# Fourth query product by Strassen's scheme in matmuls of 128 columns, in the scores' bank; another order of the products; an input ring of four

## The chip, the core and the metric

The kernel runs on one core of a Trainium2 chip. The core has a matrix engine (TensorE, "PE" in the profile; its weight loads are a row of their own, "PEld"), three engines for elementwise work (VectorE "DVE", ScalarE "ACT", GpSimd "POOL") and a queue for transfers (SyncE, "SP"). Each engine works through its own instructions in the order in which the program issues them, and waits where an instruction needs something that is not there yet. Matmuls write into eight banks of accumulators, which VectorE and ScalarE read. The metric is the device time of one execution in microseconds.

## The reference

One layer of attention with shared keys and values is added to its input. `x` is 64 batches of 128 tokens with 512 features in fp32; there are 16 heads of 64.

```python
xn = layernorm(x, g_in)
q = (xn @ Wq).reshape(b, n, H, DH).transpose(0, 2, 1, 3) * scale
kv = xn @ Wkv
k, v = (kv[..., :DH], kv[..., DH:])
...
k = jnp.concatenate([nk, k], axis=1)
v = jnp.concatenate([nv, v], axis=1)
sim = jnp.einsum('bhid,bjd->bhij', q, k)
...
sim = sim + bias
...
attn = jax.nn.softmax(sim, axis=-1)
out = jnp.einsum('bhij,bjd->bhid', attn, v)
out = out.transpose(0, 2, 1, 3).reshape(b, n, INNER)
out = out @ Wo
return layernorm(out, g_out)
```

The caller adds `x` to the result. A causal mask and a mask of keys set entries of `sim` to a large negative number, and one extra key and value (`nk`, `nv`) stand in front. The part that the change touches is `xn @ Wq`: a product of 512 features with 1024 query columns.

## The kernel before

**Groups and pairs.** Four batches make a group (`GB`), whose 512 tokens are projected together; two batches make a pair, and the main loop runs over pairs `d`. One pass of the loop is `turn(d)` and then `body(d)`; the text calls it a half, since two of them project one group. `turn(d)` makes the scores of batches 2d and 2d+1 (`scores`, L652), adds them to the bias rows (`scores_add`), and multiplies the transposed weights of the pair before with the values (`values`, L781). `body(d)` projects half of the query columns of group d // 2 + 1, runs the softmax of its pair (`exps` on ScalarE, `rinv` on VectorE, `scale` on GpSimd, `blocks_T`, a transpose on VectorE), and makes the output projection and the layer norm of earlier pairs (`out_product`, L868, `pair_norm`). `turn_end`, `body_end` and `body_last` do the last pairs. Even d is the first half of a group (h = 0) and also makes its token sums on GpSimd (`token_sum`, L497, `token_sums_inner`, L560 to 562). The order of the work is written out by hand: each engine's queue is the order of the calls.

**The query product.** The 512 x 512 blocks of weights and tokens are multiplied by Strassen's scheme in Winograd's form: seven products in place of eight (`product`, L515), each of two matmuls with 256 columns per chunk of 128 query columns. A half has two chunks, f0 and f1. Partial sums stay in accumulators: bank "a" takes products 1, 6, 7, 4 in turn (`keep` copies it out in between on ScalarE, L527), bank "c" takes 5 and 3, and `q_out` writes the queries `qT` (L536 on VectorE, L533 on ScalarE). From d = 2 on the second of the seven products is itself made by the same scheme, for both chunks of a half at once: seven matmuls of 128 columns (`inner_product`, L581, tile `pl`, in bank "w") in place of four of 256, with seven adds on VectorE (`inner_out`, L597). Its weight sums are made once, its token sums once a group.

**The values.** `values` works in four strips s of 32 rows and two halves r of columns, eight places of the array in turn. Per batch a strip does one matmul of 256 columns and three of 128. The parameter `wide` names strips that do two of the short ones as one; no call uses it.

**Banks and buffers.** Bank pair "s" (`ps_s`) holds, within a half, the scores of the first batch, then `pkv`, then a normed output row (`yn`, even batch) until `pair_residual` (L932) has read it. The input rows `x` go through a ring of `XB` = 5 tiles; the masks through two tiles, loaded by `load_mask` at h = 0.

**Start.** `q_half` and `q_batches` project the first group without Strassen's scheme; `q_batches` works batch by batch in matmuls of 128 columns. `values_T` transposes a group's values at the end of its second half, ahead of the last `exps` of the first batch.

Of the kernel before, what the change touches and what calls it, by code (L numbers as in the profile page):

```python
# [17 lines left out]
def kernel(  # L18
# [81 lines left out]
    NEG = -1.0e38  # L100
    XB = 5
    assert N == P and DH == 64 and TOK == 512
# [12 lines left out]
    def load_x(m, queue=nc.sync):  # L115
        g, t = divmod(m, GB)
        pool, tag = (rp, "res") if m in (XB, XB + 1) else (xp, "x")
        xs[m] = pool.tile([P, DIM], FP, tag=tag, name=f"x_{m}")
        if g < 2:
            queue.dma_start(out=xs[m], in_=x[m])  # L120
        else:
            nc.sync.dma_start(
                out=xs[m], in_=x[g * GB : (g + 1) * GB, t * Q : (t + 1) * Q, :]
            )

    def load_res(b):
        pool, tag = (rp, "res")
        if b >= B - 6:
# [17 lines left out]
    nkv = const.tile([P, 1], FP, name="nkv")  # L146
    nkv_neg = const.tile([P, 1], FP, name="nkv_neg")
    nbp = const.tile([P, R8], FP, name="nbp")
# [18 lines left out]
    gin_rows = const.tile([KC, P], FP, name="gin_rows")  # L167
    nc.scalar.dma_start(out=gin_rows, in_=g_in.rearrange("(kc p) -> kc p", p=P))
# [70 lines left out]

    ident = const.tile([P, P], FP, name="ident")  # L240
    make_identity(nc, ident)
# [130 lines left out]
    def null_negative():  # L372
        nc.vector.tensor_scalar(nkv_neg, nkv, -1.0, None, ALU.mult)

    def kv_pair_out(m, pkv):
# [13 lines left out]
        for at, to, n in ((0, 0, 2), (3, 2, 1), (2, 3, 1)):  # L389
# [3 lines left out]
                AF.Identity,  # L393
                bias=nkv_neg[K_ROWS],
            )
# [194 lines left out]
    def inner_out(g, h, f, t, at, name=None):  # L590
# [6 lines left out]
        nc.vector.tensor_tensor(o, p, k, ALU.add)  # L597

    S, nmax, rsum = {}, {}, {}

# [138 lines left out]
    def values_rooms_apart(p):  # L739
# [18 lines left out]
            ps_y.tile(shape, FP, tag="X", name=f"po_{p + 1}_3"),  # L758
        ]

    def values(b, wide=()):
# [194 lines left out]
    def turn(d):  # L956
# [15 lines left out]
        po = values_rooms(p)  # L972
        values(p)
        values(p + 1)
        if d % 2 and (d + 1) // 2 < NG:
# [49 lines left out]
    def body_first():  # L1025
# [19 lines left out]
        tokens_T(m)  # L1045
        load_mask(g + 1)
        for f in range(2):
# [197 lines left out]
    def body(d):  # L1245
# [8 lines left out]
        f0, f1 = 2 * h, 2 * h + 1  # L1254
        deep = q and d > 1

        if q:
# [68 lines left out]
        if q:  # L1326
            product(g, f0, 7, ps_q, "a", start=False)
            keep("a", "u3")
            q_out(g, HC + f0, 1, "c", "u3")
        if ln:  # L1330
# [5 lines left out]
        if soft:  # L1336
            scale(b, 0)
        if xw:
            norm_apply(m)
# [12 lines left out]
        if soft:  # L1352
            exps(a, 1, 0, 1)
        if q:
            product(g, f0, 4, ps_q, "a", start=False)
            q_out(g, HC + f0, 0, "a")
            product(g, f0, 3, ps_q, "c", start=False)
            q_out(g, f0, 1, "c", "u2")
# [14 lines left out]
        if soft:  # L1373
            exps(a, 1, 1, 4)
        if q:
            product(g, f1, 1, ps_q, "a")
            keep("a", "p1")
        if deep:
            inner_product(g, h, 7)
            inner_out(g, h, 1, 1, 0, "p1")  # L1380
            inner_out(g, h, 1, 1, 1)
        elif q:
            q_out(g, f1, 0, "w", "p1")
            weight_sums_inner()
        if q and h == 1:
            values_T(g)
        if soft:
# [3 lines left out]
            exps(b, 1, 0, 2)  # L1391
        if q:
            product(g, f1, 5, ps_q, "c")
        if out:
            out_product(p, 5, ps_y, "Y")
            out_keep("Y", "yp5", "yp5")
        if soft:
            exps(b, 1, 2, 3)
# [3 lines left out]
        if deep:  # L1402
            inner_product(g, h, 4)
            inner_product(g, h, 3)
            inner_out(g, h, 1, 0, 0, "p1")
            inner_out(g, h, 0, 1, 1)
        if soft:
            exps(b, 1, 3)
            blocks_T(a)
# [6 lines left out]
        if q:  # L1416
            product(g, f1, 7, ps_q, "a", start=False)
            keep("a", "u3")
            q_out(g, HC + f1, 1, "c", "u3")
        bias_add(b + 2)  # L1420
# [5 lines left out]
        if q:  # L1426
            product(g, f1, 3, ps_q, "c", start=False)
            q_out(g, f1, 1, "c", "u2")
        if out:
            pair_stats(p)  # L1430
            pair_pow(p)
            out_product(p, 7, ps_y, "X", start=False)
            out_part(p + 1, 1, "X", "yp5")
        if soft:
            blocks_T(b)
        if q:
            product(g, f1, 4, ps_q, "a", start=False)
            q_out(g, HC + f1, 0, "a")
        if out:
            out_product(p, 4, ps_y, "X", start=False)  # L1440
# [73 lines left out]
    bias_add(0, (slice(0, UK.start), slice(UK.start, ROW)))  # L1514
    q_batches((7,))
    norm_T(7)
# [104 lines left out]
```

## Time and profile before

| | |
|---|---|
| time, median of 3 runs | 1027.39 us (1027.23 to 1027.47) |
| the profiled execution's own time | 1027.63 us |
| span of its profile | 1025.8 us |
| TensorE busy | 1016.4 us |
| VectorE, ScalarE, GpSimd busy | 800.4, 697.4, 744.7 us |
| moved by DMA | 100.84 MB, 98 GB/s |

Times in the rows are microseconds from the start of the span unless marked ns. A row of a timeline gives start, length, engine, line, operation, what is written `<-` what is read, the shape, and in brackets the idle time of the engine just before it with what ended it. The ends of matmuls are modelled, and they overlap; the distance from one start to the next is what a matmul costs in a stream.

### The profile page before, as it was taken

How to read it: one execution, taken by the hardware profiler on the slowest of the kernel's cores; microseconds unless marked ns; L12 is line 12 of the kernel's file. 1: busy time of each engine (PE TensorE's matmuls, PEld its weight loads, DVE VectorE, ACT ScalarE, POOL GpSimd, SP SyncE). 2: the span in 40 equal slices, each digit the busy share in tenths (PEclk: the TensorE clock that was granted, in tenths of full speed). 3: DMA queues.
4: the chain of work that ended last, by engine and by line, in shares of the span. 5: the costliest groups of instructions: out<-in, count | busy, mean ns of one | idle time of the engine just before them, and what ended most of it. 6: DMA issues, size and time to landing. Idle time of an engine off the chain costs nothing.

```text
span 1025.8 us, 31271 instructions
## 1 busy us (share of the span) xinstructions
PE 1016.4 (99%) x12345; PEld 898.9 (88%) x12345; DVE 800.4 (78%) x1774; ACT 697.4 (68%) x2805; POOL 744.7 (73%) x579
## 2 busy tenths in 40 slices
PE   9999999999999999999999999999999999999997
PEld 9888888888888888888888888888888888888886
DVE  6877788877778877788777888777887777877697
ACT  5765678666677666786666776666776667856582
POOL 4997768676686867759677686766868678586676
PEclk9999999999999999999999999999999999999999
DMA  7415243051431414224052330514314152140211
GB/s 217 139 30 150 69 117 120 30 155 64 143 97 66 125 56 150 89 81 137 29 165 74 109 123 26 165 63 138 103 51 130 64 151 89 70 113 21 88 64 62
DMA packets 73833, 100.84 MB, mean 98 GB/s; under 512 B 32212, under 2 KB 36056, under 8 KB 71896
## 3 DMA queue, kind: packets, MB, share of 16 engines
q1 hardware_dynamic: 73392, 98.47, 30.9%
q8 instruction: 96, 1.57, 0.7%
q14 instruction: 49, 0.40, 0.1%
q10 hardware_dynamic: 296, 0.40, 0.1%
HBM read 63.19 MB, written 33.55 MB: 94 GB/s over the span
## 4 chain that ended last, share of the span: by engine, by line
PE 97%; DVE 1%; POOL 1%; issue 0%; POOLq 0%; DVEq 0%; ACT 0%
PE pa L515 20%; PE pyX L868 19%; PE pyY L868 10%; PE pc L515 10%; PE po L781 7%; PE pkv L363 6%; PE pyw L868 5%; PE pl L581 4%; PE pq L450 3%; PE ps L652 3%; PE sc_X L652 2%; PE sc_Y L652 2%; PE py_s L868 1%; PE sc_a L652 1%; PE busy L1453 1%; PE sc_w L652 1%
## 5 line engine op out<-in xcount | busy, mean ns | idle before, releaser
L683 ACT ACTIVATE s<-s,nmax 128x65 f32<-128x65 f32 (+1 forms) x1024 | 372.2, 368 | 62.1 <-DVE nmax L674 62.0
L705 POOL TENSOR_TENSOR s<-s,rinv 128x512 f32<-128x512 f32 (+1 forms) x132 | 190.6, 1446 | 159.9 <-DVE rinv L701 159.9
L617 POOL TENSOR_TENSOR s<-biasp,mneg 128x1552 f32<-128x1552 f32 (+1 forms) x65 | 206.0, 3171 | 51.1 <-DVE s L667 38.1
L683 ACT ACTIVATION_READ_ACCUMULATOR s<-s,nmax 128x1 f32 x1024 | 195.4, 191 | 0.0
L533 ACT COPY qT<-pa 128x256 f32<-128x256 f32 x59 | 22.0, 373 | 147.7 <-PE pa L515 147.7
L674 DVE TENSOR_REDUCE nmax<-s 128x8 f32<-128x1032 f32 (+1 forms) x128 | 121.4, 949 | 0.1
L515 PE MATMUL pa<-xS,wq 128*128 128x256 f32 x472 | 121.2, 379 | 0.0
L721 DVE STREAM_TRANSPOSE sb<-s 128x1536 f32<-128x1536 f32 (+1 forms) x68 | 113.5, 1672 | 2.0 <-POOL s L705 2.0
L868 PE MATMUL pyX<-wo,oT 128*128 128x256 f32 x464 | 109.7, 379 | 0.0
L868 PE MATMUL pyX<-wT,oT 128*128 128x256 f32 x464 | 109.7, 379 | 0.0
L515 PEld LDWEIGHTS pa<-xS,wq 128*128 128x128 f32 x472 | 87.3, 190 | 11.0 <-issue 0.2
L868 PEld LDWEIGHTS pyX<-wo,oT 128*128 128x128 f32 x464 | 86.0, 190 | 10.5
L868 PEld LDWEIGHTS pyX<-wT,oT 128*128 128x128 f32 x464 | 85.9, 190 | 10.6
L848 POOL TENSOR_TENSOR oT<-oT 128x512 f32<-128x512 f32 x64 | 80.5, 1276 | 3.9 <-PE pyw L868 1.6
L781 PE MATMUL po<-sb,vr 32*64 32x256 f32 (+1 forms) x4064 | 81.0, 300 | 0.0
L781 PEld LDWEIGHTS po<-sb,vr 32*64 32x64 f32 x4064 | 70.9, 130 | 8.1 <-issue 5.7
L536 DVE TENSOR_TENSOR qT<-pc,ku 128x256 f32<-128x256 f32 x118 | 48.6, 412 | 35.9 <-PE pc L515 20.8
L597 DVE TENSOR_TENSOR qT<-pl,kp 128x128 f32<-128x128 f32 x112 | 31.3, 280 | 55.5 <-PE pl L581 52.9
L800 ACT ACTIVATE oT<-po,nv 128x512 f32<-128x512 f32 (+1 forms) x127 | 73.8, 655 | 0.1
L281 POOL TENSOR_TENSOR rstd<-rstd,nhalf 128x1 f32<-128x1 f32 x64 | 35.0, 554 | 42.1 <-DVE rstd L280 39.2
L527 ACT COPY ku<-pa 128x256 f32<-128x256 f32 x118 | 43.4, 368 | 30.2 <-PE pa L515 26.2
L363 PE MATMUL pkv<-xT,wkv 128*128 128x256 f32 x256 | 63.3, 391 | 0.0
(186 smaller groups left out, 2418.9 us busy)
## 6 DMA issues: line engine op xcount, KB each, us to landing
res<-in_x_dram SPq DMA_DIRECT2D x64, 256.0 KB
x<-in_x_dram SPq DMA_DIRECT2D x63, 256.0 KB
out_dram<-y SPq DMA_DIRECT2D x63, 256.0 KB
xd<-xb SPq DMA_DIRECT2D x14, 1024.0 KB
xT<-xd SPq DMA_DIRECT2D x56, 256.0 KB
vr<-vd SPq DMA_DIRECT2D x64, 128.0 KB
kT<-kT SPq DMA_DIRECT2D x32, 64.0 KB
vd<-vb SPq DMA_DIRECT2D x32, 64.0 KB
```

The costliest lines, as they stand in the source:

```text
L363: nc.tensor.matmul(pkv, wkv[:, kc, :], xT[g][:, t : t + 2, kc, :], start=(kc == 0), stop=(kc == KC - 1),)
L515: nc.tensor.matmul(prod[tag], w[:, kc, f * P : (f + 1) * P], t[:, :, kc, :], start=(start and kc == 0), stop=(kc == HK - 1), skip_group_ch ...
L617: nc.gpsimd.tensor_tensor(S[b][:, :, keys], biasp[:, :, keys], mneg[:, t, keys] .unsqueeze(1) .broadcast_to([P, R8, keys.stop - keys.start ...
L652: nc.tensor.matmul(home[r][u * DH : (u + 1) * DH, f, :], qT[g, f, t // 2][rows, t % 2, hf, u], kT[rows, 0 : nk // Q, t, :], start=True, st ...
L674: nc.vector.tensor_reduce(nmax[b][:, hf], S[b][:, :, WITH_NULL[hf]], AX.X, ALU.max, negate=True)
L683: nc.scalar.activation(row, row, AF.Exp, bias=nmax[b][:, hf, k : k + 1], accum_out=rsum[b][:, hf, k : k + 1],)
L705: nc.gpsimd.tensor_tensor(sv, sv, rinvs[b, hf][:, lo:hi].unsqueeze(2).broadcast_to([P, hi - lo, sv.shape[2]]), ALU.mult,)
L721: nc.vector.transpose(sbs[b][:, :, lo:hi].rearrange("p j e q -> p e j q"), S[b][:, lo:hi, 1 : ROW - 1].rearrange("p e (j k) -> p e j k", k=Q),
L781: nc.tensor.matmul(po[s][rows, to : to + n], vr[g][quad, t, PLACE[j], :], sb[quad, slots, r * NF : (r + 1) * NF, :], start=(turn == 0), st ...
L800: nc.scalar.activation(to, src, AF.Identity, bias=nv2)
L848: eng.tensor_tensor(o, a, b, op)
L868: nc.tensor.matmul(prod[key], h[:, c, :], w[:, c, :], start=(start and c == 0), stop=(c == HC - 1), skip_group_check=not start,)
```

## The change

The fourth of the seven products gets the same treatment as the second, from d = 4 on (`deeper`): seven matmuls of 128 columns per half (`last_product`, tile `pm`) in place of the four of 256 of `product` 4, in the bank pair "s", which is free in that part of the body. Three weight sums lie in new tiles `wM` and `wR` (the tile `wM` first takes the fifth input row, `wR` the identity and `g_in`), the fourth overwrites a weight block; they are made at d = 2 and 3. The token sums (`token_sums_last`) are four subtractions on GpSimd per group, behind `scale(b, 0)` in the first half. In each half seven adds on VectorE (`last_out`) write the queries in place of two copies on ScalarE. `product` 1 of chunk f1 moves ahead into the place of product 4 of f0, and `product` 3 of f1 moves behind `out_product` 7. `values_T` goes behind `rinv` and `scale` of the first batch. From d = 5 on strip 3 of `values` is wide: for the first batch of a pair always, for the second at odd d and at d = 14 and 24. The input ring shrinks to four, the masks to one tile, loaded at h = 1. The last projection of the start is one `q_half`.

```diff
@@ constants and buffers
-    XB = 5
+    XB = 4
...
-        pool, tag = (rp, "res") if m in (XB, XB + 1) else (xp, "x")
-        xs[m] = pool.tile([P, DIM], FP, tag=tag, name=f"x_{m}")
+        pool, tag = (rp, "res") if m in (XB + 1, XB + 2) else (xp, "x")
+        xs[m] = wM if m == XB else pool.tile([P, DIM], FP, tag=tag, name=f"x_{m}")
...
-        m8s[g] = gp.tile([P, TOK], U8, tag="m8", name=f"m8_{g}")
+        m8s[g] = gp.tile([P, TOK], U8, tag="m8", name=f"m8_{g}", bufs=1)
...
+    wM = const.tile([P, DIM], FP, name="wM")
+    wR = const.tile([P, 2, P], FP, name="wR")
+    ident, gin_rows = wR[:, 0], wR[0:KC, 1]
@@ new functions
+    in_last = a22.rearrange("p k (h f m) -> p k f h m", h=2, f=2)
+    g11, g12 = in_last[:, 0, 0], in_last[:, 1, 0]
+    g21, g22 = in_last[:, 0, 1], in_last[:, 1, 1]
...
+    def token_sums_last(g):
+        b = xS[g, 4]
+        x = xM[g] = gp.tile([P, 3, N], FP, tag="xM", name=f"xM_{g}", bufs=1)
+        for o, p, m in (
+            (x[:, 0], b[:, 1, 0], b[:, 0, 0]),
+            (b[:, 1, 0], b[:, 1, 1], b[:, 1, 0]),
+            (x[:, 1], b[:, 1, 1], x[:, 0]),
+            (x[:, 2], b[:, 0, 1], x[:, 1]),
+        ):
+            nc.gpsimd.tensor_tensor(o, p, m, ALU.subtract)
...
+    def last_product(g, h, k):
+        if k == 1:
+            last_in[g, h] = ps_s.tile([P, 2, DIM], FP, tag="s", name=f"pm_{g}_{h}")
+        b, x = xS[g, 4], xM[g]
+        w, t, at = {
+            1: (g11, b[:, 0, 0], 0),
+            2: (g12, b[:, 0, 1], 2),
+            3: (v4, b[:, 1, 1], 1),
+            4: (g22, x[:, 2], 0),
+            5: (v1, x[:, 0], 1),
+            6: (v2, x[:, 1], 0),
+            7: (v3, b[:, 1, 0], 0),
+        }[k]
+        nc.tensor.matmul(
+            last_area(g, h, at),
+            w[:, h],
+            t,
+            start=k in (1, 2),
...
+    def last_out(g, h, f, t, at, first=False):
+        o = q_part(g, HC + 2 * h + f, 0)[:, t]
+        p = last_area(g, h, at).rearrange("p (h i) -> p h i", h=2)
+        k = o
+        if first:
+            k = base[f].rearrange("p (t h i) -> p t h i", t=2, h=2)[:, t]
+        nc.vector.tensor_tensor(o, p, k, ALU.add)
@@ turn
-        values(p)
-        values(p + 1)
+        values(p, WIDE if 4 < d < PAIRS - 1 else ())
+        values(p + 1, WIDE if 4 < d < PAIRS - 1 and (d % 2 or d % 10 == 4) else ())
@@ body
+        deeper = q and d > 3
...
-        if h == 0 and g + 1 < NG:
+        if h == 1 and g + 1 < NG:
             load_mask(g + 1)
...
+        if sums and d > 2:
+            token_sums_last(g)
...
-        if q:
+        if deeper:
+            product(g, f1, 1, ps_q, "a")
+        elif q:
             product(g, f0, 4, ps_q, "a", start=False)
             q_out(g, HC + f0, 0, "a")
...
+        if deeper:
+            last_product(g, h, 1)
+            last_product(g, h, 2)
...
-        if q and h == 1:
-            values_T(g)
+        if d == 2:
+            weight_sums_last(1, 2, 4)
         if soft:
             exps(a, 1, 4)
             rinv(a, 1)
             scale(a, 1)
             exps(b, 1, 0, 2)
+        if q and h == 1:
+            values_T(g)
...
+        if deeper:
+            last_product(g, h, 6)
+            last_product(g, h, 5)
+            last_out(g, h, 0, 1, 0, True)
...
+        if deeper:
+            product(g, f1, 3, ps_q, "c", start=False)
+            q_out(g, f1, 1, "c", "u2")
+            last_product(g, h, 3)
+            last_product(g, h, 4)
+            last_out(g, h, 1, 0, 0, True)
+            last_out(g, h, 0, 1, 1)
         if soft:
             blocks_T(b)
@@ start
-    q_batches((7,))
+    q_half(7, 0)
```

On TensorE, in the last third of `body(16)`, from the second `pyX` product to the last (`pa`, `pc` are query products of chunk f1, `pl` the inner product, `pyX`, `pyY` the output projection). Before:

```order
L868 MATMUL pyX_1_7161<-wT,oT_7076 128x256 x4
L515 MATMUL pa_1_1_7231<-xS_9_7106,wq 128x256 x2
L868 MATMUL pyY_5_7251<-wo,oT_7076 128x256 x4
L515 MATMUL pc_1_5_7248<-xT_6797,wS 128x256 x2
L868 MATMUL pyX_1_7161<-wo,oT_7076 128x256 x4
L515 MATMUL pa_1_1_7231<-xS_9_7159,wq 128x256 x2
L868 MATMUL pyX_1_7161<-wT,oT_7076 128x256 x4
```

And in the changed program:

```order
L647 MATMUL pm_0_7334<-xM_7297,wM 128x128 x2
L936 MATMUL pyX_1_7257<-wT,oT_7174 128x256 x4
L515 MATMUL pa_1_1_7312<-xS_9_7204,wq 128x256 x2
L647 MATMUL pm_0_7334<-xS_9_7255,wq 128x128
L936 MATMUL pyY_5_7351<-wo,oT_7174 128x256 x4
L936 MATMUL pyX_1_7257<-wo,oT_7174 128x256 x4
L515 MATMUL pc_1_5_7358<-xT_6888,wS 128x256 x2
L647 MATMUL pm_0_7334<-xS_9_7255,wR 128x128
L647 MATMUL pm_0_7334<-xM_7297,wq 128x128
L936 MATMUL pyX_1_7257<-wT,oT_7174 128x256 x4
```

Product 4 of f1 (`pa` from `xS_9_7159`) is gone; `pm` products 6 and 5, 7, 3 and 4 stand in between, and `pc` (product 3) and the last two `pm` are now the last ahead of the final `pyX`.

On VectorE, the end of the same half, from the second `rinv` to the last transpose. Before:

```order
L701 RECIPROCAL rinv_1_7280<-rsum_7153 128x8
L536 TENSOR_TENSOR qT_1_1_7084<-pc_1_5_7248,ku_7285 128x4x64
L898 TENSOR_TENSOR y_7197<-pyY_5_7251,kyu_7278 128x256
L536 TENSOR_TENSOR qT_1_1_7084<-pc_1_5_7248,ku_7261 128x4x64
L904 BN_STATS sto_7298<-y_7197 128x6
L906 BN_AGGR mvo_7300<-sto_7298 128x2
L908 TENSOR_SCALAR rstdo_7302<-mvo_7300 128x1
L898 TENSOR_TENSOR y_7309<-pyX_1_7161,kyp_7256 128x256
L721 STREAM_TRANSPOSE sb_7311<-s_6880 128x8x6x32
```

And in the changed program:

```order
L767 RECIPROCAL rinv_1_7386<-rsum_7249 128x8
L536 TENSOR_TENSOR qT_1_1_7182<-pc_1_5_7358,ku_7391 128x4x64
L663 TENSOR_TENSOR qT_1_0_7181<-pm_0_7334,ku_7391 128x2x64
L663 TENSOR_TENSOR qT_1_0_7181<-pm_0_7334,qT_1_0_7181 128x2x64
L966 TENSOR_TENSOR y_7293<-pyY_5_7351,kyu_7384 128x256
L972 BN_STATS sto_7404<-y_7293 128x6
L974 BN_AGGR mvo_7406<-sto_7404 128x2
L976 TENSOR_SCALAR rstdo_7408<-mvo_7406 128x1
L966 TENSOR_TENSOR y_7415<-pyX_1_7257,kyp_7356 128x256
L536 TENSOR_TENSOR qT_1_1_7182<-pc_1_5_7358,ku_7364 128x4x64
L663 TENSOR_TENSOR qT_1_0_7181<-pm_0_7334,ku_7391 128x2x64
L663 TENSOR_TENSOR qT_0_0_7179<-pm_0_7334,qT_0_0_7179 128x2x64
```

The transpose `blocks_T(b)` (L787 there) follows the last of these rows: the add of product 3 and two of the new adds, which need the last query products of the half, now stand ahead of it.

On TensorE in the changed `turn(16)`, the first batch's value products (`po_3` is strip 3):

```order
L849 MATMUL po_2_7095<-sb_6960,vr_6094 64x128 x2
L849 MATMUL po_3_7096<-sb_6960,vr_6094 64x2x128 x2
L849 MATMUL po_0_7093<-sb_6960,vr_6094 64x128 x2
L849 MATMUL po_1_7094<-sb_6960,vr_6094 64x128 x2
L849 MATMUL po_2_7095<-sb_6960,vr_6094 64x128 x2
L849 MATMUL po_0_7093<-sb_6960,vr_6094 64x128 x2
```

In the second turn strip 3 has a matmul of 2 x 128 columns, and in the third it has none.

More of the change, by code (lines that the diff above doesn't have):

```diff
@@ L597, in inner_out, with weight_sums_last, last_area @@
         nc.vector.tensor_tensor(o, p, k, ALU.add)
+    in_last = a22.rearrange("p k (h f m) -> p k f h m", h=2, f=2)
+    g11, g12 = in_last[:, 0, 0], in_last[:, 1, 0]
+    g21, g22 = in_last[:, 0, 1], in_last[:, 1, 1]
+    v1, v2 = (wM[:, i * 2 * P : (i + 1) * 2 * P] for i in range(2))
+    v1, v2 = (v.rearrange("p (h m) -> p h m", h=2) for v in (v1, v2))
+    v4, v3 = wR, g21
+    xM, last_in, base = {}, {}, {}
+    def weight_sums_last(*ks):
+        for k in ks:
+            o, p, m, op = {
+                1: (v1, g21, g22, ALU.add),
+                2: (v2, v1, g11, ALU.subtract),
+                4: (v4, g12, v2, ALU.subtract),
+                3: (v3, g11, g21, ALU.subtract),
+            }[k]
+            nc.vector.tensor_tensor(o, p, m, op)
+    def token_sums_last(g):
[8 more added lines that the diff above has]
+            nc.gpsimd.tensor_tensor(o, p, m, ALU.subtract)
+    def last_area(g, h, at):
+        two = last_in[g, h]
+        return two[:, 0, 0:N] if at == 0 else two[:, 1, (at - 1) * N : at * N]
+    def last_product(g, h, k):
[10 more added lines that the diff above has]
+            7: (v3, b[:, 1, 0], 0),
+        }[k]
+        nc.tensor.matmul(
[3 more added lines that the diff above has]
+            start=k in (1, 2),
+            stop=True,
+            skip_group_check=k not in (1, 2),
+        )
+    def last_out(g, h, f, t, at, first=False):
[5 more added lines that the diff above has]
+        nc.vector.tensor_tensor(o, p, k, ALU.add)
     S, nmax, rsum = {}, {}, {}
@@ L759, in values_rooms_apart @@
         ]
+    WIDE = (3,)
     def values(b, wide=()):
@@ L1045, in body_first @@
         tokens_T(m)
-        load_mask(g + 1)
         for f in range(2):
@@ L1374, in body @@
             exps(a, 1, 1, 4)
+        if q and not deeper:
+            product(g, f1, 1, ps_q, "a")
         if q:
-            product(g, f1, 1, ps_q, "a")
             keep("a", "p1")
+        if deeper:
+            last_product(g, h, 1)
+            last_product(g, h, 2)
         if deep:
             inner_product(g, h, 7)
+        if deeper:
+            last_out(g, h, 0, 0, 0, True)
+            last_out(g, h, 0, 0, 2)
+        if deep:
             inner_out(g, h, 1, 1, 0, "p1")
@@ L1391, in body @@
             exps(b, 1, 0, 2)
-        if q:
+        if q and h == 1:
+            values_T(g)
+        if q and not deeper:
             product(g, f1, 5, ps_q, "c")
@@ L1396, in body @@
             out_keep("Y", "yp5", "yp5")
+        if deeper:
+            product(g, f1, 5, ps_q, "c")
         if soft:
@@ L1425, in body @@
             out_part(p, 1, "Y", "yu2")
-        if q:
+        if q and not deeper:
             product(g, f1, 3, ps_q, "c", start=False)
@@ L1433, in body @@
             out_part(p + 1, 1, "X", "yp5")
+        if deeper:
+            product(g, f1, 3, ps_q, "c", start=False)
[4 more added lines that the diff above has]
+            last_out(g, h, 0, 1, 1)
         if soft:
             blocks_T(b)
-        if q:
+        if q and not deeper:
             product(g, f1, 4, ps_q, "a", start=False)
             q_out(g, HC + f1, 0, "a")
+        if d == 3:
+            weight_sums_last(3)
         if out:
```

17 lines of the change are left out of this document (11 added, 6 removed).

## The prediction

> **What bounds the kernel now.** I read the page first: busy shares, the granted clock, and the chain of work that ended last.
>
> ```profile
> span 1025.8 us, 31271 instructions
> ...
> PE 1016.4 (99%) x12345; PEld 898.9 (88%) x12345; DVE 800.4 (78%) x1774; ACT 697.4 (68%) x2805; POOL 744.7 (73%) x579
> ...
> PEclk9999999999999999999999999999999999999999
> ...
> PE 97%; DVE 1%; POOL 1%; issue 0%; POOLq 0%; DVEq 0%; ACT 0%
> ```
>
> TensorE is busy 99% of the span at full clock, and 97% of the chain is TensorE's own work. A busy share can hide waits, so the waits of TensorE come next, all of them in the whole span:
>
> ```profile
> PE py_s L868 <- DVE oT L798: 1.4, 2, 0.8
> PE busy L1453 <- POOL neg L245: 1.4, 1, 1.4
> PE pyc L868 <- DVE y L898: 0.6, 1, 0.6
> PE pc L515 <- DVE qT L536: 0.4, 1, 0.4
> ```
>
> That is 3.8 us, all at the start, in the second pair and in the last pairs. In the steady part TensorE waits for nothing. The third view cuts two consecutive halves (one `turn` plus one `body`) out of the steady part, from one start of the value products to the next, the odd d = 15 first and the even d = 16 second:
>
> ```profile
> 501.63:532.86 31.23, 31.23 (x387) 27.63 (x383) 25.00 (x57) 21.26 (x87) 21.28 (x15) 1.00 0.41 120
> 532.86:564.09 31.23, 31.23 (x387) 27.63 (x384) 24.28 (x56) 22.28 (x89) 24.00 (x22) 1.00 0.23 79
> ```
>
> The columns are length, then busy time of PE, PEld, DVE, ACT and POOL. A half lasts 31.23 us because TensorE has 31.23 us to do; VectorE has 6 to 7 us to spare in it, ScalarE 9 to 10, GpSimd 7 to 10. So a matmul taken out shortens the run by its own spacing, as long as the others still deliver in time.
>
> **The change, part by part.** The spacing is read from the even half, in order of time on TensorE. A matmul is two records, so "x4" is one product of two matmuls and "x2" one matmul; a stretch runs from one row's start to the next row's.
>
> ```profile
> 532.86 2.52 PE L781 MATMUL po<-sb,vr 32*64 32x256 f32 x128
> 535.31 1.99 PE L363 MATMUL pkv<-xT,wkv 128*128 128x256 f32 x8
> ...
> 538.00 0.38 PE L581 MATMUL pl<-xT,wq 128*128 128x128 f32 x2
> 538.22 1.89 PE L868 MATMUL pyX<-wo,oT 128*128 128x256 f32 x8
> ...
> 544.27 0.61 PE L581 MATMUL pl<-xL,wL 128*128 128x128 f32 x4
> 544.71 0.39 PE L581 MATMUL pl<-xT,wq 128*128 128x128 f32 x2
> 544.94 1.03 PE L515 MATMUL pa<-xS,wq 128*128 128x256 f32 x4
> 545.80 1.03 PE L515 MATMUL pc<-xT,wS 128*128 128x256 f32 x4
> ...
> 547.53 0.38 PE L581 MATMUL pl<-xL,wq 128*128 128x128 f32 x2
> 547.75 1.03 PE L515 MATMUL pc<-xS,wS 128*128 128x256 f32 x4
> ...
> 551.21 0.39 PE L581 MATMUL pl<-xL,wq 128*128 128x128 f32 x2
> 551.43 0.39 PE L581 MATMUL pl<-xT,wL 128*128 128x128 f32 x2
> 551.65 1.89 PE L868 MATMUL pyX<-wT,oT 128*128 128x256 f32 x8
> ...
> 558.56 1.03 PE L515 MATMUL pa<-xS,wq 128*128 128x256 f32 x4
> 559.42 1.89 PE L868 MATMUL pyX<-wT,oT 128*128 128x256 f32 x8
> ```
>
> *Term 1, the fourth product.* Removed in each half with d from 4 to 29 are product 4 of both chunks: the `pa` rows at 544.94 and 558.56, 0.86 us each, 1.72 us. Added are seven matmuls of 128 columns, which the second product already has in the same form: 0.22 (at 538.00), 0.67 for three (544.27 to 544.94), 0.22 (547.53) and 0.44 for two (551.21 to 551.65), 1.55 us. The half gets 0.17 us shorter; rows to 10 ns leave 0.17 to 0.18. Over 26 halves that is 4.4 to 4.7 us; I take 4.5.
>
> By these rows a matmul of half the columns costs half (0.22 against 0.43 us). [...]
>
> *Term 2, the wide value products.* In 41 calls of `values` (26 first batches, 15 second ones) strip 3 does two 128-column matmuls of each half of the rows as one of 256. Two matmuls fewer a call, the same columns. The two batches of the even half:
>
> ```profile
> 532.86:533.99 1.13, 1.13 (x62) 1.06 (x67) 1.00 0.32 112
> 533.99:535.31 1.32, 1.32 (x85) 1.15 (x67) 1.00 0.22 50
> ```
>
> 64 matmuls in 2.45 us are 38 ns each, so the most that two can give is 0.077 us a call, 3.1 us in all. But a strip streams 640 columns a batch, and at 0.43 us for 256 that alone is 1.08 us: the first batch (1.13) is already at its columns, and only the second (1.32, with the end of the stage in it) has something above them. The other end is a loss: if the other strips had to wait for the long matmul, 0.22 us a call. Between them I take 15 ns a call, 0.6 us in all, because the row nearest to it, the first batch, sits 0.05 us above its columns.
>
> *Term 3, the start.* The 0.4 us wait of TensorE in the second pair goes:
>
> ```profile
> L401 DVE STREAM_TRANSPOSE vb<-vT 64x512 f32<-64x512 f32 x16 | 11.3, 708 | 0.5
> 84.95 1.78 DVE L721 STREAM_TRANSPOSE sb<-s 128x1536 f32<-128x1536 f32 x1 [2.02 <-POOL s L705]
> 87.49 1.13 PE L515 MATMUL pc<-xT,wS 128*128 128x256 f32 x4 [0.45 <-DVE qT L536]
> ```
>
> There VectorE's `blocks_T(a)` waited 2.02 us for GpSimd's `scale`, which follows `rinv`, and that stood behind the 0.71 us of `values_T`. Now `rinv` goes first, and 0.45 us of lateness is less than 0.71. `q_half(7, 0)` also makes eight short matmuls into four long ones: 8 x 0.22 against 4 x 0.43, 0.05 us. I take 0.4 for both; the bounds are 0 and 0.5.
>
> *What must stay hidden.* VectorE gets seven adds a half, ScalarE loses two copies, GpSimd gets four subtractions in an even half. Two groups of instructions (mean ns of one behind the comma) and the timeline of the even half:
>
> ```profile
> L597 DVE TENSOR_TENSOR qT<-pl,kp 128x128 f32<-128x128 f32 x112 | 31.3, 280 | 55.5 <-PE pl L581 52.9 <-ACT kp L527 1.8
> L561 POOL TENSOR_TENSOR xL<-xT,xL 128x128 f32<-128x128 f32 x14 | 6.4, 457 | 1.1
> 559.10 1.77 DVE L721 STREAM_TRANSPOSE sb<-s 128x1536 f32<-128x1536 f32 x1
> 562.00 0.42 DVE L667 TENSOR_TENSOR s<-sc_w,s 128x256 f32<-128x256 f32 x1 [1.14 <-PE sc_w L652]
> 529.72 3.22 POOL L617 TENSOR_TENSOR s<-biasp,mneg 128x1552 f32<-128x1552 f32 x1 [0.84 <-DVE sb L721]
> 535.91 1.05 POOL L705 TENSOR_TENSOR s<-s,rinv 128x512 f32<-128x512 f32 x1 [0.38 <-DVE rinv L701]
> 539.20 1.27 POOL L497 TENSOR_TENSOR xS<-xT 128x512 f32<-128x512 f32 x1
> 541.68 1.03 PE L515 MATMUL pa<-xS,wq 128*128 128x256 f32 x4
> 543.68 0.69 DVE L932 TENSOR_TENSOR y<-yn,res 128x512 f32<-128x512 f32 x1
> 547.75 1.04 POOL L705 TENSOR_TENSOR s<-s,rinv 128x512 f32<-128x512 f32 x1
> ```
>
> 7 x 0.28 is 1.96 us, against 6 to 7 us of spare time on VectorE; 4 x 0.46 is 1.8 us against 7 on GpSimd. Sums are not enough, since both queues are in order, so I follow the latest piece. The last two adds stand behind products 3 and 4 of `pm`, which TensorE, in the new order, ends ahead of a last four matmuls of `pyX`: about 559.25, and 0.17 later in PSUM (a `pl` row lasts 0.39 for a spacing of 0.22). Two adds, and `blocks_T(b)`, queued behind them, starts near 559.85 instead of 559.10, 0.75 late, and ends near 561.6. VectorE's next work waits until 562.00 for the scores anyway (1.14 us of idle time there), and the value products that read the block come at 564.08. Nothing on TensorE moves. GpSimd's `bias_add` behind an odd half waits for that transpose (0.84 at 529.72) and goes 0.75 late too. The 0.38 us of idle time at 535.91 takes up half. So `token_sum(g, 3)`, ready at 540.47 now, comes near 540.85; product 7 reads it at 541.68, near 541.45 when the half is shorter. Then `scale(b, 0)` ends near 549.15 and the four new subtractions follow, 0.5 us each with their gaps: the third, which product 6 of `pm` needs, near 550.65, against 551.2 on TensorE. These two margins, 0.6 and 0.55 us, are the smallest I find, less the 0.2 us by which a weight load runs ahead. I cost the cover at 0; if it were gone, 13 even halves would pay, 1.3 us for each 0.1 us of lateness.
>
> The bank "s" is free when `pm` takes it at 546.7: its user, the normed row, is read by VectorE until about 544.4. The input ring of four frees each tile in the half before its load; the mask is loaded one half later, still more than one half ahead of its use; the weight sums are four adds in two halves. All these at 0.
>
> *Sum.* The profiled execution took 1027.63 us (span 1025.8), 0.24 above the median of 1027.39. 1027.63 - 4.5 - 0.6 - 0.4 = 1022.1, and beside the median 1021.9 us.
>
> **The rivals.** *The wide matmul holds the other strips back (slower).* Place: the second turn of each of the 41 wide calls, where one strip streams 256 columns and three stream 128. Price: up to 0.22 us a call, 9.0 us, so 1027.4 - 4.5 - 0.4 + 9.0 = 1031.5 us. It decides from 0.12 us a call. For it: this trace has no turn of mixed lengths. Against it: strips overlap freely (64 matmuls in 2.45 us), and after the long turn of strip 3 nothing of it stands in the third. [...]
>
> *GpSimd is late in even halves (no gain or slower).* Place: product 7 or product 6 of `pm`. From about 0.4 us beyond my margins the 5.5 us are gone (13 x 0.42): 1027.4 us, and 1030 at 0.6 us beyond. For it: two margins near 0.5 us in the busiest queue of that half. Against it: 7 us spare.
>
> *The softmax sets the half (no change).* If scores, maximum, exponentials, scaling and transposes took as long as a half, TensorE's saving would turn into waiting: 1027 us. Against it: TensorE shows no wait in the steady part, and VectorE idles 1.14 us for it at each turn.
>
> **How the numbers follow.** My forecast has 0.83, the wide rival 0.06, GpSimd 0.05, the softmax 0.04, anything else 0.02. The likeliest is 1021.9 us. Low end: all upper bounds, 4.7 + 3.1 + 0.5 = 8.3 under the median, 1019.1. High end: 4.4 from term 1 alone is 1023.0, and 1.5 us for waits of 0.1 us in 13 even halves make 1024.5. This holds a little over 8 in 10. A measurement of this kernel tells about 0.2% (2 us) from no change. Faster by more: my forecast and half of the GpSimd case, 0.86. Within: the softmax case and a partly paid rival, 0.06. Slower: 0.08.
>
> **What would show it.** Term 1: `pl` and the new `pm` at 0.22 us spacing, the half of d = 4, which has no wide call, near 31.05 us, and no TensorE wait in any steady half. Term 2: the value stage of an odd half under 2.45 us; above it, the wide rival. Term 3: no wait near 87 us. Cover: VectorE idle before the scores down from 1.14 to about 0.2 us. TensorE waits for GpSimd at `pa` or `pm` in even halves would prove me wrong, and so would halves of 31.2 us with waits.

## The result, and the profile after

| | before | after |
|---|---|---|
| time, median | 1027.41 us (1027.23 to 1027.51, 6 runs) | 1023.44 us (1023.20 to 1024.21, 6 runs) |
| ratio | | 0.9961 (95% interval 0.9950 to 0.9972) |
| profiled execution, span | 1027.63, 1025.8 us | 1023.20, 1021.4 us |

The change makes the kernel 4.0 us faster, 0.4%, and the interval is clear of no change; 5.5 us were forecast. The page of the changed kernel, its busy line and its queue of instruction transfers (packets, MB, share):

```profile
span 1021.4 us, 31462 instructions
...
PE 1012.7 (99%) x12333; PEld 901.1 (88%) x12333; DVE 846.5 (83%) x1960; ACT 673.1 (66%) x2753; POOL 766.5 (75%) x631
...
q8 instruction: 96, 1.57, 0.6%
```

The waits of TensorE are all at the start and the end; the 0.4 us for `qT` is gone, and no new wait for GpSimd has come (the first row stood in the kernel before too):

```profile
PE busy L1557 <- POOL neg L245: 1.4, 1, 1.4
PE py_s L936 <- DVE oT L866: 1.3, 2, 0.7
PE pyc L936 <- DVE y L966: 0.6, 1, 0.6
```

Four halves of the steady part, d = 15 to 18 (columns as in the prediction), and the value stages that open them:

```profile
499.28:530.36 31.08, 31.08 (x385) 27.74 (x381) 26.72 (x64) 20.29 (x85) 20.35 (x15) 1.00 0.42 118
530.36:561.72 31.36, 31.35 (x388) 27.61 (x384) 26.01 (x63) 21.32 (x87) 26.58 (x26) 1.00 0.25 81
561.72:592.80 31.08, 31.08 (x384) 27.74 (x381) 26.72 (x64) 20.30 (x85) 20.36 (x15) 1.00 0.43 122
592.80:623.89 31.09, 31.09 (x388) 27.73 (x385) 25.96 (x63) 21.32 (x87) 26.56 (x26) 1.00 0.25 78
```

```profile
499.28:501.75 2.47, 2.47 (x125) 2.22 (x121) 2.47 (x4) 2.47 (x15) 1.95 (x1) 1.00 0.02 7
530.36:533.11 2.75, 2.74 (x128) 2.11 (x124) 2.75 (x4) 2.75 (x16) 2.67 (x3) 1.00 0.28 103
561.72:564.19 2.47, 2.47 (x125) 2.23 (x121) 2.47 (x4) 2.47 (x15) 1.98 (x1) 1.00 0.02 7
592.80:595.28 2.48, 2.48 (x129) 2.23 (x125) 2.48 (x4) 2.48 (x15) 2.40 (x3) 1.00 0.31 90
```

A half went from 31.225 to 31.08 us. In the kernel before, every value stage up to d = 29 was 2.450 us; now the odd ones are 2.466, the even ones 2.479, and d = 16 stands out with 2.753. TensorE's busy time shows nothing of that: 2.74 of 2.75. The weight loads do. Stage d = 16, then d = 18:

```profile
530.36 0.23 PEld L849 LDWEIGHTS po<-sb,vr 32*64 32x64 f32 x16 [0.17 <-issue]
531.06 1.88 PEld L849 LDWEIGHTS po<-sb,vr 32*64 32x64 f32 x108 [0.47 <-issue]
...
592.80 2.31 PEld L849 LDWEIGHTS po<-sb,vr 32*64 32x64 f32 x124 [0.17 <-issue]
```

At d = 16 the loads stop after 16 for 0.47 us, with nothing that they wait for ("issue"). The 0.17 us ahead of a stage is in all of them. Smaller gaps of this kind stand at d = 2 (stage 2.589) and d = 4 (2.573), where no call is wide.

From the starts of the value stages in the two traces, the gain of the profiled executions is put together thus:

| part | worked out from | us |
|---|---|---|
| fourth product | e1's undisturbed halves, 31.065, against 31.225: 26 x 0.160 | +4.2 |
| wide value products | 15 stages +0.016, 10 stages +0.029 | -0.53 |
| `values_T` moved, `q_half` | distances at 86 us (below), 0.71 + 0.05 | +0.76 |
| stages that ran dry | d = 2, 4, 16: 0.139 + 0.123 + 0.274 | -0.54 |
| first projection begins at 8.86 in place of 9.12 us | differs from run to run | +0.26 |
| sum, to the last stage (cumulative shift 4.20) | | +4.1 |

The spans differ by 4.4; the last 0.2 us lie behind the last stage. The row on the first projection is no gain of the change: in e5, which has the kernel before but for one later line, it begins at 8.92 us, and in the other experiments at 8.80 to 9.00. The spacing of the very first matmuls is part of it at most: it falls from 0.213 to 0.112 us at 7.55 us in the trace before, at 6.88 here, and already at 5.06 in e2, where the projection begins at 8.96. What else moves it stays open.

**The dry places.** The queue q8 moved 96 packets of 16.4 KB (1.57 MB / 96). TensorE has 24,848 records in the trace (its 12,333 matmul records, as many loads, and some 180 waits), 259 a packet, and the packets come three to a half, as the 768 records of a half on average do: by these counts its instructions come in blocks of 256. Counting records from the start, the loads of d = 2, 4 and 16 stop at record 1985, 3521 and 12737: each 193 records into a block. That is a hypothesis from three points; the experiments test it.

The traces also tie the stops to q8. From d = 2 to 29, the value stages and the projections `pkv` behind them have 27 stops of over 0.2 us in the traces of the changed kernel and the experiments. In each, the load that comes late starts 1.2 to 1.6 us after the end of a q8 packet. In the kernel before, which has no such stop, the last packet had ended 2.0 us or more ahead of the same load.

### The profile page after: what moved, and what is told of

Same layout as the page of the kernel before. It is cut to its first block, busy times and chain, and to the rows that moved or that the text cites. A ratio compares the mean times of both kernels' runs of the same rounds, so it can differ in the third digit from the quotient of the medians.

```text
span 1021.4 us, 31462 instructions
## 1 busy us (share of the span) xinstructions
PE 1012.7 (99%) x12333; PEld 901.1 (88%) x12333; DVE 846.5 (83%) x1960; ACT 673.1 (66%) x2753; POOL 766.5 (75%) x631
## 3 DMA queue, kind: packets, MB, share of 16 engines
q8 instruction: 96, 1.57, 0.6%
## 4 chain that ended last, share of the span: by engine, by line
PE 97%; DVE 1%; POOL 1%; issue 0%; POOLq 0%; DVEq 0%
PE pyX L936 20%; PE pa L515 16%; PE pyY L936 10%; PE pc L515 10%; PE po L849 8%; PE pkv L363 6%; PE pyw L936 5%; PE pl L581 4%; PE pm L647 4%; PE pq L450 3%; PE ps L718 3%; PE sc_X L718 2%; PE sc_Y L718 2%; PE py_s L936 1%; PE sc_a L718 1%; PE sc_w L718 1%
## 5 line engine op out<-in xcount | busy, mean ns | idle before, releaser
L787 DVE STREAM_TRANSPOSE sb<-s 128x1536 f32<-128x1536 f32 (+1 forms) x68 | 113.7, 1674 | 11.2 <-POOL s L771 11.1
L964 ACT COPY y<-pyX 128x256 f32<-128x256 f32 x29 | 10.8, 373 | 167.5 <-PE pyX L936 136.0
L849 PE MATMUL po<-sb,vr 32*64 32x128 f32 (+1 forms) x3904 | 82.1, 308 | 0.0
L515 PE MATMUL pa<-xS,wq 128*128 128x256 f32 x264 | 67.8, 380 | 0.0
L515 PE MATMUL pa<-xT,wq 128*128 128x256 f32 x236 | 60.7, 380 | 0.0
```

The source lines that it names most:

```text
L515: nc.tensor.matmul(prod[tag], w[:, kc, f * P : (f + 1) * P], t[:, :, kc, :], start=(start and kc == 0), stop=(kc == HK - 1), skip_group_ch ...
L787: nc.vector.transpose(sbs[b][:, :, lo:hi].rearrange("p j e q -> p e j q"), S[b][:, lo:hi, 1 : ROW - 1].rearrange("p e (j k) -> p e j k", k=Q),
L849: nc.tensor.matmul(po[s][rows, to : to + n], vr[g][quad, t, PLACE[j], :], sb[quad, slots, r * NF : (r + 1) * NF, :], start=(turn == 0), st ...
```

## The experiments

Times are medians; the kernel before had 1027.52 or 1027.53 us beside each of these. "Place" is the record at which a value stage begins, counted from 1 at the start of the program, modulo 256. Without wide calls, scores and values together are 512 records in 5.3 us, the rest of a half 256 records in 26 us.

### e1: no wide calls

```diff
-        values(p, WIDE if 4 < d < PAIRS - 1 else ())
-        values(p + 1, WIDE if 4 < d < PAIRS - 1 and (d % 2 or d % 10 == 4) else ())
+        values(p)
+        values(p + 1)
```

> No call of the value products is wide any more, so TensorE's records per half go from 768 on average back up to 781 (12 for the three matmuls more, at four records each). Theory F (blocks): TensorE's instructions come in blocks of 256 records (96 transfers of 16.4 KB on queue q8 for 24,666 matmul and load records in the changed kernel); its loads ran dry at d = 2, 4 and 16 at the same record modulo 256, so what counts is where a block ends relative to the 512 dense records of scores and values. With 13 records of drift a half the block end passes through all places, and many stages run dry: 0.05 to 0.4 us each, 2 to 5 us in all, 1025 to 1028 us, while stages that do not run dry go back to 2.450 us. Rival P (the price of the wide matmul alone counts): every value stage is 2.450 us, 0.56 us less than in the changed kernel in all, 1022.9 us. By the prediction's second term, which gave a wide call a gain of 15 ns, it would be 0.6 us more, 1024.0 us, with stages longer than the wide ones.

Measured: 1029.16 us (1027.21 to 1030.68), ratio 1.0017 (1.0008 to 1.0025): slower than before the change. Waits of the loads and of TensorE, and d = 8, the worst stage:

```profile
PEld sc_Y L718 <- issue: 10.1, 31, 0.3
PEld po L849 <- issue: 10.1, 42, 1.1
PEld pkv L363 <- issue: 2.5, 13, 0.5
...
PE po L849 <- issue: 1.9, 4, 0.9
```

```profile
282.74 2.25 PEld L849 LDWEIGHTS po<-sb,vr 32*64 32x64 f32 x124 [0.17 <-issue]
286.11 0.19 PEld L849 LDWEIGHTS po<-sb,vr 32*64 32x64 f32 x4 [1.12 <-issue]
```

Each half against an undisturbed one (31.065 us; 31.226 up to d = 4), by the place of its stage:

| place | 150-154 | 166-180 | 192-206 | 218-254 | 14-50 | 66-102 | 118-144 |
|---|---|---|---|---|---|---|---|
| halves | d = 2, 3, 4, 24 | 5, 6, 25, 26 | 7, 8, 27, 28 | 9 to 12, 29 | 13 to 16 | 17 to 20 | 21 to 23 |
| lost, us | 0.14, 0, 0.68, 0 | 0, 0, 0, 0 | 0.44, 1.28, 0.01, 0.75 | 0.15, 0.39, 0.24, 0, 0.02 | 0.22, 0.08, 0.12, 0.55 | 0.66, 0.38, 0.38, 0.33 | 0, 0, 0.19 |

17 halves lose 7.0 us in all, and the stops above 0.2 us all stand 193 records into a block (at d = 7 in `pkv`, behind the stage). The first row of the waits is something else: the loads idle 0.33 us within the scores of every half, in every trace and at every place. Theory F holds; its sum was put too low (2 to 5). So the wide calls, which cost 0.53 us by themselves, make the kernel 5.7 us faster (1029.16 - 1023.44): they take out 12 of the 13 records a half that the fourth product adds, and keep the stages at places that do not run dry. Without them the change would have been a loss.

### e2 and e3: 16 records more, 16 fewer, ahead of everything

```diff
e2
-    q_half(7, 0)
+    q_batches((7,))
e3
-    q_batches((6,))
+    q_half(6, 0)
```

> The last projection of the start goes back to eight short matmuls, 0.05 us dearer, 16 records more ahead of everything. Theory F: the value stages of d = 2 and d = 4 lie 16 records later in their block, where those of the kernel before lay, and run 2.450 us without a gap; d = 16 too; 0.54 us of gaps go, so about 0.4 us faster than the changed kernel, 1023.0 us, unless the later stages, now up to 192 records into the block, run dry at their other end. Rival N (the gaps come from other traffic at that time and not from the place in the block): gaps of 0.1 to 0.3 us stay at d = 2, 4 and 16 or come at other stages, 1023.5 us.

> The projection before it becomes four long matmuls too: 16 records fewer ahead of everything, 0.05 us less work. Theory F: every value stage starts 134 to 160 records into its block, where the block after next is asked for only when the dense scores have begun; nearly all of 30 stages run dry by 0.1 to 0.3 us, 3 to 8 us in all, 1026 to 1031 us, from four matmuls less. Rival N: 1023.4 us, with at most three or four stages longer than 2.48 us.

e2: 1023.15 us (1022.88 to 1023.29), ratio 0.9956 (0.9943 to 0.9970). Its stages stand at places 166 to 192. d = 2 and d = 4 ran 2.452 us. The loads of d = 4, without a gap now:

```profile
157.28 2.28 PEld L849 LDWEIGHTS po<-sb,vr 32*64 32x64 f32 x128 [0.17 <-issue]
```

In the changed kernel that row was 2.40 us long. But d = 16 kept its gap (2.804), so that one is not the place alone (e8).

e3: 1026.56 us (1025.38 to 1028.42), ratio 0.9992 (0.9983 to 1.0001): four matmuls fewer at the start, and the gain over the kernel before is gone. Eight stages ran dry by 0.33 to 0.64 us, 3.7 us in all; seven are even ones. The sum was as forecast, but by fewer and longer stops: the odd halves run at these places too, and only d = 15 of them was hit.

### e4: the value transposes back in their place

```diff
         elif q:
             q_out(g, f1, 0, "w", "p1")
             weight_sums_inner()
+        if q and h == 1:
+            values_T(g)
...
-        if q and h == 1:
-            values_T(g)
```

> The value transposes go back ahead of the first batch's last exponentials. TensorE's wait in the second pair comes back. By the waits' row of the kernel before it costs 0.4 us, as the prediction had it: 1023.8 us. By the distances between matmuls around it in that trace (0.826 and 0.320 us in place of 0.216 each) it costs 0.71 us, since the weight load behind the wait isn't ahead any more: 1024.15 us. If later groups are delayed by the same transposes, further waits appear in odd halves, more than 1024.5 us.

Measured: 1024.47 us (1024.02 to 1024.95), ratio 0.9970 (0.9958 to 0.9981). The matmuls around the place in e4, and in the changed kernel:

```profile
84.89 1.89 PE L936 MATMUL pyY<-wo,oT 128*128 128x256 f32 x8
87.22 1.13 PE L515 MATMUL pc<-xT,wS 128*128 128x256 f32 x4 [0.44 <-DVE qT L536]
```

```profile
84.84 1.89 PE L936 MATMUL pyY<-wo,oT 128*128 128x256 f32 x8
86.56 1.03 PE L515 MATMUL pc<-xT,wS 128*128 128x256 f32 x4
```

From `pyY` to `pc` it is 2.33 against 1.72 us, 0.61, and `pc` is 0.10 longer: 0.71 us for a wait that its view gives as 0.4. The half from d = 1 to 2 is 32.101 against 31.389 us, the same 0.71. No further wait came. The rest of the 1.03 us between the medians fits larger gaps: in this trace, of the slowest of the six executions, 0.49 and 0.67 us at d = 2 and d = 4, against 0.14 and 0.12.

### e5: the kernel before, four matmuls fewer

```diff
-    q_batches((7,))
+    q_half(7, 0)
```

> The kernel before, with only its last projection of the start as four long matmuls in place of eight short ones: 16 records fewer and 0.05 us less work ahead of everything, none of the other parts of the change. Theory F (blocks): its value stages, 166 or 169 records into their block in every half, go to 150 and 153, where e3 had gaps of 0.35 to 0.65 us in most even halves (whose refill stands behind the token transfers) and none in odd ones; 8 to 14 of the 15 even halves pay, 3 to 8 us, 1030 to 1035 us. Rival (the gaps belong to the new products or to the wide matmuls): 1027.35 to 1027.45 us, every half 31.225 us.

Measured: 1031.04 us (1030.71 to 1033.16), ratio 1.0038 (1.0025 to 1.0051): 3.5 us lost by taking out 0.05 us of work, with nothing of the change but this line. Places 150 and 153. Stage d = 12, then d = 11:

```profile
408.80 0.63 PEld L781 LDWEIGHTS po<-sb,vr 32*64 32x64 f32 x22 [0.17 <-issue]
409.70 1.79 PEld L781 LDWEIGHTS po<-sb,vr 32*64 32x64 f32 x106 [0.27 <-issue]
...
377.57 2.28 PEld L781 LDWEIGHTS po<-sb,vr 32*64 32x64 f32 x128 [0.17 <-issue]
```

Nine even halves up to d = 28 lost 0.12 to 0.59 us, 2.9 in all; d = 30 lost 0.17; no odd half lost any. Stages run dry without the new products and the wide matmuls.

### e6: the second batch wide in place of the first

To e2, in the even halves with one wide call:

```diff
-        values(p, WIDE if 4 < d < PAIRS - 1 else ())
-        values(p + 1, WIDE if 4 < d < PAIRS - 1 and (d % 2 or d % 10 == 4) else ())
+        values(p, WIDE if 4 < d < PAIRS - 1 and (d % 2 or d % 10 == 4) else ())
+        values(p + 1, WIDE if 4 < d < PAIRS - 1 else ())
```

> Against e2 (1023.15 us): in the 11 even halves with one wide call, the second batch's values are wide and not the first's; the same count of records everywhere. If the two calls' prices add up (first +28 ns by the halves with only that one wide, both together +16, so the second -12), these stages go from 2.480 to about 2.440 us, 0.44 us less in all, 1022.7 us. If the price hangs on a change between wide and plain batches, they stay at 2.48 us or get longer, 1023.15 us or more. The prediction's second term (both gain 15 ns) had them at 2.435 us.

Measured: 1022.69 us (1022.61 to 1022.87), ratio 0.9953 (0.9940 to 0.9965), 0.46 below e2. Stage d = 12, with only its second batch wide:

```profile
405.64:408.08 2.44, 2.44 (x128) 2.19 (x125) 2.44 (x4) 2.44 (x15) 2.36 (x3) 1.00 0.28 90
```

To the nanosecond it is 2.438: first batch +0.028, second -0.012, and the two add up. There are ten such halves, not the eleven of the expectation, since `turn` runs to d = 29; by the stages they make 0.41 us. The prediction had given both a gain of 0.015.

### e7: GpSimd one microsecond later

To e2: the first of the four new token subtractions is made three times.

```diff
             (x[:, 0], b[:, 1, 0], b[:, 0, 0]),
+            (x[:, 0], b[:, 1, 0], b[:, 0, 0]),
+            (x[:, 0], b[:, 1, 0], b[:, 0, 0]),
```

> Against e2: GpSimd makes the first of its four new subtractions three times in each of the 13 even halves, 2 x 0.48 us more ahead of the sum that product 6 of pm reads. By the prediction's margin of 0.55 us (in e2's trace the third sum ends 0.57 us ahead, less the 0.34 us of that half's gap) TensorE waits 0.4 to 0.7 us for GpSimd at pm in each even half, 5 to 9 us in all, 1028 to 1032 us. If the cover is wider than an added 1 us, no wait, 1023.2 us.

Measured: 1029.76 us (1029.54 to 1030.83), 6.6 above e2.

```profile
PEld pm L649 <- POOL xM L629: 5.4, 10, 0.6
...
PE pm L649 <- POOL xM L629: 3.5, 10, 0.4
```

Product 6 of `pm`, where the prediction put the margin, is the place. In the ten even halves that wait, its first matmul starts 0.60 to 0.66 us after the one ahead of it (0.11 in e2), so it is 0.5 us late; the half as a whole is 0.59 to 0.66 us longer. In the other three (d = 4, 16 and 28) it is 0.11 us late at most, where all 13 were forecast to wait. That is 6.2 us in ten halves, for waits that TensorE's row gives as 3.5. Added were 1.0 us, so the margin was about 0.5.

### e8: VectorE's instructions moved against its blocks

To e2, at d = 1 to 4:

```diff
         scores(b, 1, ((ps_y, "X"), (ps_q, "c")))
+        for _ in range(7 if d < 5 else 0):
+            nc.vector.tensor_scalar(gin8[:, 0:1], gin8[:, 0:1], 1.0, None, ALU.mult)
         scores_add(a, 0)
```

> Against e2: 28 one-column instructions on VectorE, seven ahead of the scores' adds in each of the halves d = 1 to 4, where VectorE waits for the scores anyway. Theory V: the gap of 0.3 us that is left at d = 16 begins with a block of VectorE's own instructions, whose transfer on q14 falls between the last bytes of the tokens' store and its completion at d = 13 and 15, so that the tokens' loads start 0.5 and 1.2 us late, drain late, and TensorE's block comes late. VectorE uses about 138 records in two halves, 10 more than a block of 128, so 28 records move the meeting about two or three groups earlier: at d = 13 and 15 the loads come 3.9 us after the store again, the gap at d = 16 goes, and another one or none stands at d = 8, 10 or 12: 1022.85 to 1023.15 us. If it is the program's place or data at d = 15, nothing moves, with the gap of 0.3 us still at d = 16.

The reason for it: in an undisturbed even half of the changed kernel the first packet of q8 runs 3.0 to 3.6 us ahead of the value stage, just as the tokens' loads drain; at d = 16 it runs 1.8 us ahead (and 1.8 and 1.9 us at d = 2 and 4, the other two dry stages). At d = 16 the transfer engines are still full, as their share (the column before the last) shows for the time from 3.5 to 2.0 us ahead of the stages of d = 16 and d = 18:

```profile
526.86:528.36 1.50, 1.50 (x60) 1.14 (x62) 1.29 (x2) 0.37 (x1) 0.21 (x1) 1.00 1.06 309
589.30:590.80 1.50, 1.50 (x60) 1.14 (x62) 1.29 (x2) 0.37 (x1) 0.21 (x1) 1.00 0.67 153
```

and the loads there (`xT<-xd`) began late after the store that they wait for, at d = 15 and then as usual at d = 17:

```profile
514.97 0.33 SPq L335 DMA_DIRECT2D xd<-xb  x1
520.06 1.76 SPq L343 DMA_DIRECT2D xT<-xd  x4
...
577.41 0.33 SPq L335 DMA_DIRECT2D xd<-xb  x1
581.30 1.75 SPq L343 DMA_DIRECT2D xT<-xd  x4
```

Store to load, us, in the 14 groups:

```
before 3.80 3.89 3.84 3.84 3.83 3.89 3.84 3.83 3.85 3.90 3.84 3.83 3.85 3.89
after  3.88 3.94 3.90 3.91 3.89 3.95 4.39 5.10 3.89 3.96 3.90 3.90 3.89 3.94
e2     3.85 3.94 3.90 3.90 3.90 3.95 4.36 5.09 3.89 3.96 3.90 3.91 3.90 3.94
e8     3.87 3.93 3.89 4.39 4.35 3.94 3.90 3.90 3.89 3.96 3.88 3.90 3.90 3.94
```

In the two late groups of the changed kernel a packet of the queue q14 (kind "instruction" in the profile; 8,192 bytes, half of one of q8, so 128 records by estimate; 0.31 us) runs 3.7 us after the store. The last of 16 packets of 4 bytes, behind which the loads begin, runs at 3.69 and 4.00 us, against 3.49 in the other groups.

e8 measured 1022.95 us (1022.69 to 1023.31), ratio 0.9955 (0.9941 to 0.9969). The late groups moved from d = 13 and 15 to 7 and 9, three groups earlier, and the stage of d = 16 ran 2.479 us. Theory V holds for the place. Both late groups are now 0.5 us late, and the stages behind them lost nothing, like that of d = 14 in the changed kernel; only the one that was 1.2 us late did. In the time e8 can't be told from e2, since at d = 1 the added instructions themselves cost 0.18 us and a gap of 0.15 came at d = 31.

### e9: e6 and e8 together

> e6 with 28 one-column instructions on VectorE at places where it waits anyway (10 in the first group's body, 6 ahead of the scores' adds at d = 2, 3 and 4), so that VectorE's block does not meet the tokens' store at d = 15. Theories F and V together: no value stage above 2.480 us from d = 2 to 29 but where a shifted meeting still costs one gap; the gap at d = 16 (0.65 us in e6's trace, 0.3 in e2's) goes: 1022.1 to 1022.5 us, below e6's 1022.69 and both kernels. If the added instructions cost as much as the gap, as at d = 1 in e8 (0.18 us), 1022.7 us.

e6 with six such instructions ahead of the scores' adds at d = 2, 3 and 4 and ten in the first group's body. Measured: 1022.23 us (1022.15 to 1022.86), ratio 0.9948 (0.9935 to 0.9962), the fastest of all: 1.2 us below the change, 5.3 below the kernel before. No stage from d = 2 to 29 is above 2.467 us, the loads' row is back at the figure of the kernel before, and the half of d = 16 no longer stands out beside that of d = 17:

```profile
PEld po L849 <- issue: 5.7, 32, 0.3
```

```profile
530.15:561.20 31.05, 31.05 (x388) 27.66 (x385) 25.99 (x63) 21.32 (x87) 26.55 (x26) 1.00 0.24 78
561.20:592.28 31.08, 31.08 (x385) 27.70 (x381) 26.71 (x64) 20.28 (x85) 20.34 (x15) 1.00 0.43 123
```

## Why the prediction was right, and where it was not

The direction and the range were right, and the main term was: the bound (TensorE busy for 1012.7 of 1021.4 us), the spacings of `pl` and `pm` (0.22 us for two matmuls, 0.111 and 0.112 for one), the absence of new waits. The forecast of 1021.9 us missed the median by 1.5, and the second of its three terms had the wrong sign, the third the wrong size.

- *Term 1, the fourth product* (4.5 us). Right in mechanism, a little large: 0.160 to 0.163 us a half against 0.17 read from rows to 10 ns, 4.2 us in all where its bounds were 4.4 to 4.7. The half of d = 4 was 31.184 us with its gap of 0.123, so 31.06 (forecast 31.05).
- *Term 2, the wide value products* (+0.6). The step that failed. The sign was wrong: 0.53 us lost, +0.028 for a first batch and -0.012 for a second (e6). The calls were miscounted by one, too: 40, not 41, since the last `turn` is d = 29 (e1 has 160 more matmul records, four for each call). Worse, "two matmuls fewer" was read as time, where what counted was the number of instructions. The rival with a loss of up to 0.22 us a call named the right direction, at an eighth of its price.
- *What the sum had no term for.* Where TensorE's blocks of instructions end. It costs 0.5 us in the changed kernel, and would have cost 7.0 without the wide calls (e1). The page before had shown both halves of it: 12,345 matmul records and as many loads, and a queue of 96 instruction packets. Counted from stage to stage, waits included, its halves have 771 and 765 records by turns, 1536 for two, six blocks exactly, so each stage stood 166 or 169 records into its block. The 12 records that three matmuls more add, and the 8 that a wide call takes away, could have been counted from the diff.
- *Term 3, the start* (0.4, bounds 0 to 0.5). Right in place, too small: 0.76. A wait of 0.45 us in the row is 0.71 in the distances of starts (e4): in the trace before, the weight load of the first matmul behind the wait starts with it, at 87.49 us, where the next loads start 0.21 us ahead of their matmuls. The bounds had taken the row's figure as the ceiling.
- *The cover.* Right. VectorE's idle time ahead of the scores went from 1.14 to 0.21 us (forecast about 0.2), in the changed kernel at d = 17:

```profile
559.64 0.42 DVE L733 TENSOR_TENSOR s<-sc_w,s 128x256 f32<-128x256 f32 x1 [0.21 <-PE sc_w L718]
```

  The margin for product 6 of `pm`, put at 0.55 us, is about 0.5 by e7. Had it been gone, 0.1 us of lateness in 13 halves would have cost a little more than the 1.3 us that were put: half a microsecond of lateness cost 0.6 a half.
- *The softmax rival* did not occur: no wait, and halves of 31.08.

By its parts the change is worth 4.2 - 0.53 + 0.76 - 0.54 = 3.9 us against 5.5 forecast; the medians differ by 3.97. The range of 1019.1 to 1024.5 held the time, but its low end rested on a gain of the wide calls that isn't there, and nothing in it covered the 1029 us of the same change without them. That the time fell inside it is in part luck: the wide calls pay by the count of instructions, which the prediction did not look at.

What stays open: in which records exactly a block is asked for, which block that is (the block after next, in the expectation of e3, was the author's assumption), and why at equal places some halves lose 0.1 and others 0.6 us. That the tokens' loads decide it in even halves is shown for d = 16 (e8, e9) and argued for the others from odd halves being spared (e3, e5); d = 15, the odd stage that e3 did lose time in, is not explained by it. Which engine's packet sits on q14 was inferred from VectorE's record count and borne out by e8, not seen.

## What to carry to other kernels

Where an engine is busy 99% of the span, count its instructions as well as its time: here 13 records more a half (e1) moved every later stretch against the blocks of 256 in which the instructions arrive, and the dense stretch (512 records in 5.3 us) paid, with 7.0 us in 17 halves. An edit that looks useless (here matmuls merged at a loss of 0.53 us, which make the kernel 5.7 us faster) may be there for the count; try a change with and without some instructions far ahead of it before it is judged. Price a wait by the distance between the starts around it, not by the waits' row (here 0.71 us against 0.45).

## What was not expected of the hardware

- TensorE ran out of instructions with nothing that its loads waited for, which cost 0.1 to 1.28 us a half; the stops above 0.2 us from d = 2 to 29 all stood 193 records into a block of 256. In the profile such a stop is an idle time of the weight loads with "issue" behind it (0.47 us at d = 16), while the matmuls, whose ends are modelled, count as busy (2.74 of 2.75 us there). Idle times marked "issue" that every half has (0.17 us ahead of the values, 0.33 in the scores) are not such stops.
- Sixteen records (four matmuls) taken out ahead of the main loop cost 3.5 us in the kernel before (e5) and 3.1 in the changed one (e3).
- An instruction packet of 8 KB, 0.3 us long, on the queue q14 (taken for VectorE's from e8) delayed TensorE. Where it met the end of a store, the last 4-byte packet came 0.2 and 0.5 us late, and the loads behind it 0.5 and 1.2. Behind the later one TensorE's packet on q8 came late too (it began 1.8 us ahead of the stage, in place of 3.0 to 3.6), and so a stage by 0.27 to 0.65 us (d = 16 in the changed kernel, e2, e4 and e6); with the meeting moved, that was gone (e8, e9).
- A strip's long matmul among short ones costs 28 ns in the first of two batches and gains 12 in the second (stages of 2.450 us without one, 2.479 with the first, 2.438 with the second, 2.466 with both).
